# A block's edge products in one four-bank tile, with longer VectorE operations, in a graph layer with gathers

## The chip, the cores and the metric

The kernel runs on one core of a Trainium2 chip. A core has engines that run side by side, each with its own queue of instructions: TensorE (PE, matrix products; its weight loads are shown as PEld), VectorE (DVE), ScalarE (ACT), GpSimd (POOL) and SyncE (SP, which issues transfers). They wait for one another through semaphores. SBUF is the working memory; PSUM holds what PE writes, in eight banks of 512 float32 per partition. Transfers between HBM and SBUF run on 16 DMA engines. The metric is device time in microseconds (us), lower is better.

## The reference

All is float32. There are 8192 nodes of 256 features, 131072 edges with 64 attributes each, sorted by their target node, and groups of 32 nodes for attention (4 heads of 64).

```python
ea  = edge_attr @ w_e + b_e                       # 131072 x 256
msg = relu(x[src] + ea)
agg = segment_sum(msg, dst, num_segments=8192)
t   = x + agg
h_local = bn1(relu(t @ w1 + b1) @ w2 + b2 + x)
q, k, v = split(x.reshape(256, 32, 256) @ in_w.T + in_b)
attn    = softmax(q @ k.T / 8)                    # per group of 32 and head
h_attn  = bn2((attn @ v) @ out_w.T + out_b + x)
out = h_local + h_attn
out = bn3(out + relu(out @ m_w1 + m_b1) @ m_w2 + m_b2)
result = layernorm(x + out)
```

## The kernel before, in words

The edges are cut into 128 blocks of 1024 (`NB`, `BE`), the nodes into 16 chunks of 512 (`NCH`, `CH`). Blocks are numbered in the order of their edges, so block b mostly adds into the nodes around 64 b.

For a block, `gather` (L152 to L163) issues eight indirect transfers on POOL, each of which fetches 128 rows of x by the edges' source numbers into one of four buffers `xs`; it is called two blocks ahead. For the first 20 blocks (`NX`) the rows come from x itself, and PE adds the bias b_e by products with `sel` (L203); later they come from `xb`, a copy of x with b_e added. That copy is made on DVE by `copy_stream` (L639 to L647), one addition `xp` of 256 elements per partition at a time (L643), in the gaps that `copy_some` fills while the first 16 or so blocks run.

`edge_transpose` (L190) turns the edge attributes on DVE. `edge_products` (L195) multiplies them with w_e into PSUM tiles `pe` of two banks; a block needs two such tiles, one for each pair of 256-edge groups, and there are two buffers. `edge_messages` (L219) adds the gathered rows on DVE (L229, one operation of 1024 elements per tile) and takes the relu on ACT (L233). `edge_hot` (L236) compares node offsets with a row of numbers and so makes matrices of zeros and ones, in two operations of 128 elements (L241); `edge_sums` multiplies them with the messages (L250), ACT copies the sums (L268), and a second compare makes `oh2` (L279, one operation per block); `edge_place` multiplies again (L290) and adds the sums to the node tiles `xT` (L299).

The node work is written as generators. `attention_front` and `attention_back` make q, k, v, the scores, the softmax and the output of a chunk. The scores go into two tiles `pe` of the same two buffers (L482, L486); eight copies on ACT bring them to SBUF (L496). Softmax subtracts the maximum in four operations of 128 elements (L505) and multiplies with the reciprocal in four more (L512). `dense` makes the rest of a chunk: w1, w2 with an update of `hA` on DVE (L568), m_w1, m_w2, transposes and the layer norm.

The order on PE is written out by hand. Until block 104 (`TAIL`) a loop takes two blocks at a time: products and messages of the first, sums of the two blocks before, products and messages of the second, `edge_place`, and node work in between, handed out by `Work.run` by stated costs and by what is ready. From block 26 (`NV`) on, node work also stands between the sums and the second block's products; until then DVE and ACT follow the written order too, and later the scheduler orders them. From block 104 on a small planner (L803 to L855) goes block by block with an assumed time `came` at which a block's rows arrive, and picks what comes next. Its last block is taken in pieces: `first_sums` sums three of its four groups early, the last addition is cut in two, and the last `ws` copy in two halves on two engines.

At the end a check of `width` decides whether a slow general path runs; with these inputs it doesn't.

Of the kernel before, what the change touches and what calls it, by code (L numbers as in the profile page):

```python
# [24 lines left out]
NH = 4  # L25
# [47 lines left out]
def gnn_kernel(ctx: ExitStack, tc: tile.TileContext, x, src, dst, edge_attr, w, out):  # L73
# [72 lines left out]
    def bank2():  # L146
        return pps.tile([P, 2, CH], FP, name="pe", tag="pe", bufs=2)
# [47 lines left out]
    def edge_products(b):  # L195

        eaT = eaT_of.pop(b).rearrange("p (h m) r -> p h (m r)", h=NH)
        for h in range(0, NH, 2):
            pe = bank2().rearrange("p i (u c) -> p i u c", u=2)
            half = [slice(i * ED, (i + 1) * ED) for i in range(2)]  # L200
            if b < NX:
                for i, rows in enumerate(half):
                    nc.tensor.matmul(  # L203
                        pe[:, i], sel[rows, :], be[rows, None, :].to_broadcast([ED, 2, C]), start=True, stop=False, skip_group_check=True
                    )
            for u in range(2):
                for i, rows in enumerate(half):
                    nc.tensor.matmul(  # L208
                        pe[:, i, u, :], eaT[rows, h + u], we[rows, :], start=(b >= NX), stop=True, skip_group_check=True
                    )  # L210
            pe_of[b, h] = pe
# [7 lines left out]
    def edge_messages(b):  # L219

        xs = xs_of.pop(b)
        msg = msg_of[b] = epool.tile([P, NH, TJ, C], FP, name="msg", tag="msg", bufs=3)
        n = 2 if b < NB - 1 else 1
        for h in range(0, NH, 2):
            pe = pe_of.pop((b, h))
            for u in range(0, 2, n):
                hs = slice(h + u, h + u + n)
                for js in [slice(0, TJ)] if n == 2 or h + u < NH - 1 else [slice(j, j + 1) for j in range(TJ)]:
                    nc.vector.tensor_add(  # L229
                        msg[:, hs, js].rearrange("p u i c -> p i u c"), pe[:, js, u : u + n, :],  # L230
                        xs[:, hs, js].rearrange("p u i c -> p i u c"),
                    )
                    nc.scalar.activation(msg[:, hs, js], msg[:, hs, js], AF.Relu)  # L233
        between()

    def edge_hot(b):  # L236

        oh = oh_of[b] = epool.tile([P, TB, WN], FP, name="oh", tag="oh", bufs=2)
        for t0 in range(0, TB, TB // 2):
            ts = slice(t0, t0 + TB // 2)  # L240
            nc.vector.tensor_tensor(  # L241
                oh[:, ts],
                iota_n[:, None, :WN].to_broadcast([P, TB // 2, WN]),
                rel[:, b, ts, None].to_broadcast([P, TB // 2, WN]),
                ALU.is_equal,
            )
# [8 lines left out]
    def first_sums(b):  # L255
        pw = pps.tile([P, 2, C], FP, name="pw", tag="pw", bufs=1)
        group_sums(pw, 0, b, [(h, j) for h in range(NH - 1) for j in range(TJ)])
        return pw

    def edge_sums(blocks, pw=None):  # L260

        n, ws = len(blocks), []
        if pw is None:
            pw = pps.tile([P, 2, C], FP, name="pw", tag="pw", bufs=1)
            for i, b in enumerate(blocks):
                group_sums(pw, i, b, [(h, j) for j in range(TJ) for h in range(NH)])
            ws = epool.tile([P, 2, C], FP, name="ws", tag="ws", bufs=2)
            newest["ws"] = nc.scalar.copy(ws[:, :n], pw[:, :n]).ins  # L268
            ws = [ws[:, :, k * P : (k + 1) * P] for k in range(KC)]
        else:  # L270
            group_sums(pw, 0, blocks[0], [(NH - 1, j) for j in range(TJ)])
            for k, copy in enumerate((nc.vector.tensor_copy, nc.scalar.copy)):
                half = epool.tile([P, 2, C], FP, name="ws", tag="ws", bufs=2)
                copy(half[:, 0, :P], pw[:, 0, k * P : (k + 1) * P])
                ws.append(half[:, :, :P])
        oh2 = epool.tile([P, 2, WB], FP, name="oh2", tag="oh2")
        for i, b in enumerate(blocks):
            wn = window(b)
            nc.vector.tensor_scalar(oh2[:, i, :wn], iota_n[:, :wn], wrow[:, b : b + 1], None, ALU.is_equal)  # L279
        return blocks, ws, oh2  # L280

    def edge_place(blocks, ws, oh2):
# [4 lines left out]
        for i, b in enumerate(blocks):  # L287
            at, wn = first_node(b) - n, window(b)
            for k in range(KC):
                nc.tensor.matmul(  # L290
                    l2[:, k, at : at + wn], ws[k][:, i, :], oh2[:, i, :wn],
                    start=(i == 0 and k == 0), stop=(i == last), skip_group_check=True,
                )
# [168 lines left out]
    def attention_back(st, pool, bank, bank2):  # L462
# [40 lines left out]
        parts = [slice(a, a + H) for a in range(0, TN * H, H)]  # L503
        for q in parts:
            nc.vector.tensor_sub(pr3[:, q], pr3[:, q], mx[:, q, None].to_broadcast([P, H, NPG]))  # L505
# [5 lines left out]
        for q in parts:  # L511
            nc.vector.tensor_mul(pr3[:, q], pr3[:, q], sm[:, q, None].to_broadcast([P, H, NPG]))  # L512
# [126 lines left out]
    def copy_stream(i):  # L639
        for _, c, n in steps[i] if 0 <= i < len(steps) else []:  # L640
            xp = xp_of[c]
            for r in range(n * TN):
                nc.vector.tensor_add(xp[:, r, :], xp[:, r, :], be)  # L643
# [78 lines left out]
    with tc.manual_schedule(engines={PE}):  # L722
# [9 lines left out]
        for c in range(NCH):  # L732
# [10 lines left out]
            work.add(BACK, lambda s=st: s.get("front"), attention_back(st, npool, bank, bank2))  # L743
# [62 lines left out]
        summed_at, bank_free, first = {}, t, None  # L806
        work.at = [t] * len(work.streams)
        while l < NB:
# [51 lines left out]
    with tc.If(wide > 0):  # L860
# [67 lines left out]
        with tc.tile_pool(name="gfin", bufs=1) as pool, tc.tile_pool(name="gfin_ps", bufs=1, space=PSUM) as ps_pool:  # L928
# [4 lines left out]
            def gbank2():  # L933
                return ps_pool.tile([P, 2, CH], FP, name="gat2", tag="gat2", bufs=2)

            with tc.For_i(0, N, CH) as n0:
# [3 lines left out]
                for _ in attention_back(st, pool, gbank, gbank2):  # L940
# [39 lines left out]
```

## Time and profile before

| | us |
|---|---|
| median of 3 runs (1315.16 to 1317.74) | 1316.08 |
| the profiled execution | 1315.55 |
| its span, first to last instruction | 1313.8 |
| busy: PE / DVE / ACT / POOL | 1195.3 / 803.0 / 592.0 / 975.1 |

The profile is one execution. A row of the timeline gives the start and the length of an instruction (or of several equal ones, x4), its engine and line, what it writes and reads, and in square brackets the idle time of its engine before it and what ended that. A row of a group gives the count, the busy time, the mean length of one in ns, and the idle time before them. "Issue" is time in which an engine waited for nothing that the profile shows. Lengths of matmuls are modelled and overlap.

### The profile page before, as it was taken

Reading aid. Unit: us, or ns where it says so; the run is one execution under the profiler, and the core shown is the slowest. Engines: PE = TensorE matmul, PEld = TensorE weight load, DVE = VectorE, ACT = ScalarE, POOL = GpSimd, SP = SyncE. Lnnn points to the kernel's source line nnn. Section 1 sums busy time; section 2 is a strip of 40 time slices with the busy share of each in tenths; the row PEclk is TensorE's granted clock in tenths of the full one; section 3 lists DMA queues with packets and bytes.
Section 4 is the critical chain, followed back from the end, with each engine's and each line's share of the span. In section 5 each row is a group of like instructions: output and inputs, shape, how many; then the busy total and the mean of one; then the engine's idle time right before and its main releaser. Section 6 shows DMA issues by size and latency. Waiting matters only on the chain.

```text
span 1313.8 us, 21074 instructions
## 1 busy us (share of the span) xinstructions
PE 1195.3 (91%) x7683; PEld 720.5 (55%) x7683; DVE 803.0 (61%) x1635; ACT 592.0 (45%) x850; POOL 975.1 (74%) x1032
## 2 busy tenths in 40 slices
PE   5987989999999979998997998889898999989986
PEld 3544645556565545555554554545555555545664
DVE  5567665757566565755646574555647558475663
ACT  2524444454545264444544444353454445453443
POOL 6777777777777777777777777777777777777772
PEclk8988999999999999898999999989899999999999
DMA  9999985667666666756766666666667567666741
GB/s 234 287 315 281 274 219 167 178 182 194 172 176 167 170 177 161 190 160 155 195 161 184 164 177 169 157 181 171 170 169 191 147 170 196 160 167 155 193 134 50
DMA packets 148922, 240.35 MB, mean 183 GB/s; under 512 B 27950, under 2 KB 112204, under 8 KB 148044
## 3 DMA queue, kind: packets, MB, share of 16 engines
q0 software_dynamic: 49152, 134.28, 38.5%
q1 hardware_dynamic: 98572, 104.65, 29.4%
q8 instruction: 62, 1.02, 0.3%
q14 instruction: 48, 0.39, 0.1%
q10 hardware_dynamic: 1088, 0.00, 0.0%
HBM read 222.06 MB, written 16.78 MB: 182 GB/s over the span
## 4 chain that ended last, share of the span: by engine, by line
POOL 38%; PE 26%; issue 17%; DMA 9%; DVE 7%; ACT 2%; SPq 0%; DVEq 0%; POOLq 0%; ACTq 0%
POOL xs L157 38%; PE at L558 8%; DMA xs<-xb,srci 6%; PE pe L208 5%; PE pw L250 3%; PE at L455 2%; DVE msg L229 2%; PE pe L203 2%; PE l L290 2%; DMA xs<-in_x_dram,srci 2%; PE at L536 1%; DVE bd L516 1%; PE at L524 1%; PE at L469 1%; DVE y L601 1%
## 5 line engine op out<-in xcount | busy, mean ns | idle before, releaser
L157 POOL DMA_INDIRECT xs<-xb,srci x864 | 820.1, 949 | 263.2 <-issue 250.1
L233 ACT ACTIVATE msg<-msg 128x1024 f32<-128x1024 f32 (+1 forms) x259 | 269.9, 1046 | 399.2 <-DVE msg L229 395.2
L229 DVE TENSOR_TENSOR msg<-pe,xs 128x1024 f32<-128x1024 f32 (+1 forms) x259 | 306.5, 1205 | 198.0 <-PE pe L208 87.8
L208 PE MATMUL pe<-we,eaT 64*128 64x256 f32 x2048 | 266.1, 396 | 14.3 <-ACT pr L496 10.6
L208 PEld LDWEIGHTS pe<-we,eaT 64*128 64x128 f32 x2048 | 192.8, 191 | 117.6 <-issue 61.7
L157 POOL DMA_INDIRECT xs<-in_x_dram,srci x144 | 138.1, 959 | 43.9 <-issue 40.5
L250 PE MATMUL pw<-msg,oh 128*32 128x256 f32 x2048 | 130.9, 383 | 1.8 <-ACT msg L233 1.3
L558 PE MATMUL at<-hA,mw 128*128 128x512 f32 (+2 forms) x320 | 125.3, 520 | 4.8 <-DVE hA L568 4.8
L455 PE MATMUL at<-xT,inT 128*128 128x512 f32 x256 | 121.1, 599 | 3.2 <-ACT xT L445 3.2
L558 PE MATMUL at<-m,mw 128*128 128x512 f32 (+2 forms) x320 | 119.4, 517 | 0.0
L190 DVE STREAM_TRANSPOSE eaT<-ea 128x512 f32<-128x512 f32 x128 | 89.9, 702 | 22.7 <-PE pe L208 18.7
L250 PEld LDWEIGHTS pw<-msg,oh 128*32 128x32 f32 x2048 | 60.4, 109 | 64.9 <-issue 22.2
L290 PEld LDWEIGHTS l<-oh,ws 128*128 128x128 f32 x512 | 73.2, 194 | 27.4 <-issue 20.8
L290 PE MATMUL l<-oh,ws 128*128 128x160 f32 (+4 forms) x512 | 85.3, 306 | 2.4 <-ACT ws L268 1.6
L558 PEld LDWEIGHTS at<-hA,mw 128*128 128x128 f32 x320 | 55.0, 192 | 53.2 <-issue 41.2
L558 PEld LDWEIGHTS at<-m,mw 128*128 128x128 f32 x320 | 55.7, 193 | 48.0 <-issue 45.0
L455 PEld LDWEIGHTS at<-xT,inT 128*128 128x128 f32 x256 | 46.7, 190 | 57.3 <-issue 46.6
L458 ACT ACTIVATE qk<-at,vec 128x512 f32<-128x512 f32 x64 | 43.8, 685 | 73.3 <-PE at L455 73.2
L574 ACT ACTIVATE m<-at,vec 128x512 f32<-128x512 f32 (+2 forms) x80 | 47.9, 599 | 58.6 <-PE at L558 58.2
L558 PE MATMUL at<-xT,w 128*128 128x512 f32 (+2 forms) x160 | 66.0, 548 | 8.8 <-DVE xT L299 8.8
L558 PE MATMUL at<-h,w 128*128 128x512 f32 (+2 forms) x160 | 66.8, 542 | 7.6 <-ACT oT L531 5.5
L241 DVE TENSOR_TENSOR oh<-iota_n,rel 128x128 f32<-128x128 f32 x256 | 57.7, 278 | 17.7 <-PE pw L250 17.6
(113 smaller groups left out, 1199.7 us busy)
## 6 DMA issues: line engine op xcount, KB each, us to landing
ea<-in_edge_attr_dram SPq DMA_DIRECT2D x512, 128.0 KB
xs<-xb,srci POOLq DMA_INDIRECT x864
xn<-in_x_dram SPq DMA_DIRECT2D x16, 512.0 KB
out_dram<-y SPq DMA_DIRECT2D x14, 512.0 KB
xp<-in_x_dram SPq DMA_DIRECT2D x10, 512.0 KB
xb<-xp SPq DMA_DIRECT2D x10, 512.0 KB
xp<-in_x_dram SPq DMA_DIRECT2D x3, 1024.0 KB
xb<-xp SPq DMA_DIRECT2D x3, 1024.0 KB
```

What stands on the lines that cost most here:

```text
L157: nc.gpsimd.indirect_dma_start(out=xs[:, h, j, :], out_offset=None, in_=x if b < NX else xb[:, :], in_offset=bass.IndirectOffsetOnAxis(ap= ...
L190: nc.vector.transpose(eaT, ea[:, QR:].rearrange("p (g d) -> p g d", d=ED)[:, :, :QR])
L208: nc.tensor.matmul(pe[:, i, u, :], eaT[rows, h + u], we[rows, :], start=(b >= NX), stop=True, skip_group_check=True)
L229: nc.vector.tensor_add(msg[:, hs, js].rearrange("p u i c -> p i u c"), pe[:, js, u : u + n, :], xs[:, hs, js].rearrange("p u i c -> p i u c"),
L233: nc.scalar.activation(msg[:, hs, js], msg[:, hs, js], AF.Relu)
L241: nc.vector.tensor_tensor(oh[:, ts], iota_n[:, None, :WN].to_broadcast([P, TB // 2, WN]), rel[:, b, ts, None].to_broadcast([P, TB // 2, WN ...
L250: nc.tensor.matmul(pw[h * WN : (h + 1) * WN, i, :], oh_of[b][:, h * TJ + j, :], msg_of[b][:, h, j, :], start=(j == 0), stop=(j == TJ - 1), ...
L290: nc.tensor.matmul(l2[:, k, at : at + wn], ws[k][:, i, :], oh2[:, i, :wn], start=(i == 0 and k == 0), stop=(i == last), skip_group_check=True,
L455: nc.tensor.matmul(ps, inT[:, k, o * P : (o + 1) * P], xT[:, k, :], start=(k == 0), stop=(k == KC - 1))
L458: nc.scalar.activation(qk[:, o, :], ps, AF.Identity, bias=v_("in_b", o))
L558: nc.tensor.matmul(ps, wt[:, k, o * P : (o + 1) * P], act[:, k, :], start=(k == 0), stop=(k == nk - 1))
L574: nc.scalar.activation(m1[:, o, :], layer(mw1, KC, o, hA), AF.Relu, bias=v_("m_b1", o))
```

## The change

- `bank2`, a tile of two banks in two buffers, becomes `bank4`, a tile of four banks in one buffer. A block's products fill it whole; the scores of a chunk use the same tile.
- `edge_messages` adds and takes the relu of a block in one operation each of 2048 elements (the last block still by groups).
- `edge_hot` makes its compare in one operation of 256 elements. The compare for `oh2` covers both blocks of a pair in one operation with two inputs from SBUF, a `tensor_tensor`, where a `tensor_scalar` per block stood.
- Softmax's subtraction and multiplication are one operation of 512 elements each.
- The copy to `xb` adds the bias to 1024 elements at a time. `copy_some` and `between` still take one step at a call.
- In the tail `first_sums` is gone: the last block's products are issued in two halves, one before and one after the placing of the block ahead of it; its sums are issued together, its `ws` is copied at once, and its times in the planner are others.

Since readiness and stated costs decide what node work comes next, some of that work changes place on PE as well.

```diff
-    def bank2():
-        return pps.tile([P, 2, CH], FP, name="pe", tag="pe", bufs=2)
+    def bank4():
+        return pps.tile([P, 4, CH], FP, name="pe", tag="pe", bufs=1)
...
-    def edge_products(b):
-        eaT = eaT_of.pop(b).rearrange("p (h m) r -> p h (m r)", h=NH)
-        for h in range(0, NH, 2):
-            pe = bank2().rearrange("p i (u c) -> p i u c", u=2)
+    def edge_products(b, pairs=range(0, NH, 2)):
+        eaT = eaT_of[b].rearrange("p (h m) r -> p h (m r)", h=NH)
+        if b not in pe_of:
+            pe_of[b] = bank4().rearrange("p (i k) (u c) -> p i (k u) c", i=2, u=2)
+        pe = pe_of[b]
+        for h in pairs:
...
-        n = 2 if b < NB - 1 else 1
-        for h in range(0, NH, 2):
-            pe = pe_of.pop((b, h))
-            for u in range(0, 2, n):
-                hs = slice(h + u, h + u + n)
+        pe = pe_of.pop(b)
+        for hs in [slice(0, NH)] if b < NB - 1 else [slice(h, h + 1) for h in range(NH)]:
...
-        for t0 in range(0, TB, TB // 2):
-            ts = slice(t0, t0 + TB // 2)
-            nc.vector.tensor_tensor(
-                oh[:, ts],
-                iota_n[:, None, :WN].to_broadcast([P, TB // 2, WN]),
-                rel[:, b, ts, None].to_broadcast([P, TB // 2, WN]),
-                ALU.is_equal,
-            )
+        nc.vector.tensor_tensor(
+            oh,
+            iota_n[:, None, :WN].to_broadcast([P, TB, WN]),
+            rel[:, b, :, None].to_broadcast([P, TB, WN]),
+            ALU.is_equal,
+        )
...
-        for i, b in enumerate(blocks):
-            wn = window(b)
-            nc.vector.tensor_scalar(oh2[:, i, :wn], iota_n[:, :wn], wrow[:, b : b + 1], None, ALU.is_equal)
+        b, wn = blocks[0], max(window(b) for b in blocks)
+        nc.vector.tensor_tensor(
+            oh2[:, :n, :wn],
+            iota_n[:, None, :wn].to_broadcast([P, n, wn]),
+            wrow[:, b : b + n, None].to_broadcast([P, n, wn]),
+            ALU.is_equal,
+        )
...
+        four = bank4()
         for hh in range(H // 2):
-            two = bank2()
+            two = four[:, 2 * hh : 2 * hh + 2]
...
-        parts = [slice(a, a + H) for a in range(0, TN * H, H)]
-        for q in parts:
-            nc.vector.tensor_sub(pr3[:, q], pr3[:, q], mx[:, q, None].to_broadcast([P, H, NPG]))
+        nc.vector.tensor_sub(pr3, pr3, mx[:, :, None].to_broadcast([P, TN * H, NPG]))
...
-        for q in parts:
-            nc.vector.tensor_mul(pr3[:, q], pr3[:, q], sm[:, q, None].to_broadcast([P, H, NPG]))
+        nc.vector.tensor_mul(pr3, pr3, sm[:, :, None].to_broadcast([P, TN * H, NPG]))
...
-            for r in range(n * TN):
-                nc.vector.tensor_add(xp[:, r, :], xp[:, r, :], be)
-                if r == n * TN - 1:
+            for r in range(n):
+                xr = xp[:, r * TN : (r + 1) * TN, :]
+                nc.vector.tensor_add(xr, xr, be[:, None, :].to_broadcast([P, TN, C]))
+                if r == n - 1:
...
-                    times[1] = max(came[s] - 0.4, bank_free) if first is None else came[s] + 1.2
-            if p < NB and m == p:
+                    times[1] = max(came[s] + 2.2, bank_free)
+            if p < NB - 1 and m == p:
...
-                times[3] = came[m] - (2.4 if m == NB - 1 else 0.0)
+                times[3] = came[m]
...
-            elif t >= times[1] and s == NB - 1 and first is None:
-                first = first_sums(s)
-                t += 0.8
+                if l == NB - 1:
+                    edge_products(l, [2])
+                    edge_hot(l)
+                    t += 1.0
+                    p += 1
             elif t >= times[1]:
-                sums = edge_sums([s], first)
-                t += 1.2 if first is None else 0.3
+                sums = edge_sums([s])
+                t += 1.2
                 summed_at[s] = t
                 s += 1
+                if s == NB - 1:
+                    edge_products(s, [0])
+                    t += 1.0
```

More of the change, by code (lines that the diff above doesn't have):

```diff
@@ L193, in gnn_kernel @@
     pe_of, msg_of, oh_of, newest = {}, {}, {}, {}
-    def edge_products(b):
-        eaT = eaT_of.pop(b).rearrange("p (h m) r -> p h (m r)", h=NH)
-        for h in range(0, NH, 2):
-            pe = bank2().rearrange("p i (u c) -> p i u c", u=2)
-            half = [slice(i * ED, (i + 1) * ED) for i in range(2)]
+    def edge_products(b, pairs=range(0, NH, 2)):
[3 more added lines that the diff above has]
+        pe = pe_of[b]
+        half = [slice(i * ED, (i + 1) * ED) for i in range(2)]
+        for h in pairs:
             if b < NX:
@@ L253, in group_sums, with edge_sums @@
             )
-    def first_sums(b):
+    def edge_sums(blocks):
+        n = len(blocks)
         pw = pps.tile([P, 2, C], FP, name="pw", tag="pw", bufs=1)
[L257 to L264, printed above, removed]
-            for i, b in enumerate(blocks):
[L266 to L275, printed above, removed]
-        oh2 = epool.tile([P, 2, WB], FP, name="oh2", tag="oh2")
-        for i, b in enumerate(blocks):
-            wn = window(b)
-            nc.vector.tensor_scalar(oh2[:, i, :wn], iota_n[:, :wn], wrow[:, b : b + 1], None, ALU.is_equal)
+        for i, b in enumerate(blocks):
+            turns = [(h, j) for j in range(TJ) for h in range(NH)]
+            group_sums(pw, i, b, sorted(turns) if b == NB - 1 else turns)
+        ws = epool.tile([P, 2, C], FP, name="ws", tag="ws", bufs=2)
+        newest["ws"] = nc.scalar.copy(ws[:, :n], pw[:, :n]).ins
+        oh2 = epool.tile([P, 2, WB], FP, name="oh2", tag="oh2")
+        b, wn = blocks[0], max(window(b) for b in blocks)
[4 more added lines that the diff above has]
+            ALU.is_equal,
+        )
         return blocks, ws, oh2
```

32 lines of the change are left out of this document (15 added, 17 removed).

## The prediction

> **What bounds the kernel now.** I read the page first (busy shares, the 40 slices, the costliest groups), then POOL's own instructions in the timeline, then who POOL waits for, and only then the stretches around the edited lines.
>
> ```profile
> PE 1195.3 (91%) x7683; PEld 720.5 (55%) x7683; DVE 803.0 (61%) x1635; ACT 592.0 (45%) x850; POOL 975.1 (74%) x1032
> ...
> POOL 6777777777777777777777777777777777777772
> ...
> L157 POOL DMA_INDIRECT xs<-xb,srci x864 | 820.1, 949 | 263.2 <-issue 250.1
> ```
>
> PE shows the largest share, but POOL is the engine whose slices never change: seven tenths in every slice from the second to the last but one. Its 1024 gathers are one row of work, and what lies between them is "issue", not a wait. The first and the last gather in the timeline, and POOL's waits:
>
> ```profile
> 4.39 1.10 POOL L157 DMA_INDIRECT xs<-in_x_dram,srcd  x1 [2.80 <-issue]
> ...
> 1289.18 0.94 POOL L157 DMA_INDIRECT xs<-xb,srci  x1 [0.30 <-issue]
> ```
> ```profile
> POOL xs L157 <- issue: 297.7, 969, 2.8
> ...
> POOL xs L157 <- DVE msg L229: 2.1, 7, 0.3
> ```
>
> From 4.39 to 1289.18 are 1284.8 us for 1023 steps. An undisturbed step is 0.95 us of work and 0.30 us of issue, 1.25 us; 1023 of them make 1278.8. So the span of 1313.8 is 4.4 us of start, 1278.8 us of gathers at full rate, 6.0 us by which single gathers ran long, and 24.6 us from the last gather's start to the end. The longest wait of POOL for a message buffer is 0.3 us, which is the issue gap itself: no buffer ever held it up. Work taken off DVE, ACT or PE in the body is therefore worth nothing by itself; the time moves only through (a) gathers that run long, (b) a buffer that comes free too late, (c) the tail.
>
> **(a) Which gathers run long.** Rows of the timeline, DVE and POOL, in pairs:
>
> ```profile
> 54.94 0.42 DVE L643 TENSOR_TENSOR xp<-xp,be 128x256 f32<-128x256 f32 x1
> 55.15 1.03 POOL L157 DMA_INDIRECT xs<-in_x_dram,srci  x1 [0.30 <-DVE msg L229]
> ...
> 82.17 0.42 DVE L643 TENSOR_TENSOR xp<-xp,be 128x256 f32<-128x256 f32 x1
> 82.28 1.14 POOL L157 DMA_INDIRECT xs<-in_x_dram,srci  x1 [0.30 <-issue]
> ...
> 185.52 0.42 DVE L643 TENSOR_TENSOR xp<-xp,be 128x256 f32<-128x256 f32 x1
> 185.74 1.02 POOL L157 DMA_INDIRECT xs<-in_x_dram,srci  x1 [0.30 <-issue]
> ...
> 858.20 0.90 DVE L505 TENSOR_TENSOR pr<-pr,mx 128x128 f32<-128x128 f32 x4
> 858.70 1.01 POOL L157 DMA_INDIRECT xs<-xb,srci  x1 [0.30 <-issue]
> ...
> 1262.07 1.23 DVE L229 TENSOR_TENSOR msg<-pe,xs 128x1024 f32<-128x1024 f32 x1 [0.47 <-DMA xs<-xb,srci]
> 1262.95 0.94 POOL L157 DMA_INDIRECT xs<-xb,srci  x1 [0.30 <-issue]
> ```
>
> And the DVE groups by shape:
>
> ```profile
> L229 DVE TENSOR_TENSOR msg<-pe,xs 128x1024 f32<-128x1024 f32 x254 | 303.6, 1218 | 196.9 <-PE pe L208 87.8 <-DMA xs<-xb,srci 60.4 <-ACT m L574 15.6
> L241 DVE TENSOR_TENSOR oh<-iota_n,rel 128x128 f32<-128x128 f32 x256 | 57.7, 278 | 17.7 <-PE pw L250 17.6
> L643 DVE TENSOR_TENSOR xp<-xp,be 128x256 f32<-128x256 f32 x64 | 24.6, 417 | 0.0
> L279 DVE TENSOR_SCALAR oh<-iota_n,wrow 128x160 f32<-128x160 f32 x80 | 21.8, 310 | 0.0
> L505 DVE TENSOR_TENSOR pr<-pr,mx 128x128 f32<-128x128 f32 x64 | 14.6, 283 | 0.3
> L512 DVE TENSOR_TENSOR pr<-pr,sm 128x128 f32<-128x128 f32 x64 | 14.6, 287 | 0.4
> L229 DVE TENSOR_TENSOR msg<-pe,xs 128x512 f32<-128x512 f32 x3 | 2.0, 683 | 0.1
> ```
>
> From 512 to 1024 elements L229 grows by 0.535 us, 1.045 ns an element; 256 elements stream for 0.27 us. The L643 of 82.17 is done streaming at about 82.47 (0.27 and some 0.03 of start). The gather that starts inside it, at 82.28, is 0.19 us longer than 0.95: it waits until just then. The same sum gives 0.09 and 0.08 for the pairs at 55.15 and 185.74, and 0.08 and 0.07 were seen. Over the trace, 15 gathers start inside an L643 (first and last above), 14 of them over 0.03 us late, 0.12 us on average; the four pieces of L505 at 858.20 do it too. The L229 at 1262.07 has one input in PSUM, and the gather inside it takes 0.94: none of the 222 that start inside an L229 is late. So a gather that begins while DVE streams an operation with both inputs in SBUF waits for that operation's end. An operation that streams for L catches a start with chance L/1.25 and then costs L/2 on average: L²/2.5. For L643 that is 64 x 0.27²/2.5 = 1.9 us, against 15 x 0.12 = 1.8 seen.
>
> [...]
>
> **The change, part by part.** Cost goes with L², so k operations merged into one cost k times as much:
> - The copy to xb: 64 of 256 become 16 of 1024 elements, L 1.07: 16 x 1.07²/2.5 = 7.3, in place of 1.9: +5.5 us, all by block 16.
> - Softmax's subtraction and multiplication: 128 of 128 become 32 of 512, L 0.535: 3.7 in place of 0.9: +2.7.
> - The compare for oh: 256 of 128 become 128 of 256: 3.7 in place of 1.8: +1.9.
> - The compare for oh2: a tensor_scalar per block becomes a tensor_tensor with two SBUF inputs, for 51 pairs of about 300 elements (L 0.31) and 26 single blocks of about 110: 2.1, in place of about 0.4 seen at L279: +1.7.
>
> Sum +11.8. No two-SBUF operation of 512 or 1024 elements is in this trace. Below: a hit costs what it costs now whatever L is; the copy's 14 hits (16 x 1.07/1.25) then cost 0.12 each, softmax's 14, oh's 27 and oh2's 14 about 0.08 each, 6.1 in all where 5.0 stand now: +1. Above: every start inside waits out the full L, twice the mean: 33.6 in place of 5.0, +29. The rows lie on the line of "until the end" to 0.02 us, so I take +11.8; where the hits fall is chance, some 2 us either way.
> - The message addition and relu: one of 2048 in place of two of 1024, 2.29 and about 1.9 us. One input is in PSUM, so no gather pays. DVE saves 0.15 us a block, hidden.
>
> **(b) Buffers.** One tile of four banks means that the next block's products wait for the whole addition. Rows of PE, DVE, ACT and POOL in the stretch where PE is the late engine:
>
> ```profile
> 82.19 3.68 PE L524 MATMUL at<-bd,vn 128*64 128x128 f32 x32 [6.34 <-DVE bd L516]
> ...
> 95.93 1.23 DVE L229 TENSOR_TENSOR msg<-pe,xs 128x1024 f32<-128x1024 f32 x1 [0.50 <-DMA xs<-in_x_dram,srci]
> ...
> 97.68 1.13 PE L203 MATMUL pe<-be,sel 64*128 64x512 f32 x4
> ...
> 153.87 2.06 PE L486 MATMUL pe<-qk 64*128 64x128 f32 x32
> ...
> 155.08 3.00 ACT L496 COPY pr<-pe 32x256 f32<-32x256 f32 x8 [5.04 <-PE pe L486]
> ...
> 156.62 1.13 PE L203 MATMUL pe<-be,sel 64*128 64x512 f32 x4 [0.69 <-ACT pr L496]
> ...
> 184.38 1.23 DVE L229 TENSOR_TENSOR msg<-pe,xs 128x1024 f32<-128x1024 f32 x1 [0.50 <-PE pe L208]
> ...
> 187.06 0.95 POOL L157 DMA_INDIRECT xs<-in_x_dram,srci  x1 [0.30 <-DVE oh L279]
> ...
> 201.49 1.22 DVE L229 TENSOR_TENSOR msg<-pe,xs 128x1024 f32<-128x1024 f32 x1 [0.44 <-PE pe L208]
> ...
> 207.13 0.95 POOL L157 DMA_INDIRECT xs<-xb,srci  x1 [0.30 <-issue]
> ```
>
> A gather needs the buffer of four blocks before. Block 14's last addition ends at 185.61 and the gather of block 18 starts at 187.06: 1.45 us to spare, the least of all blocks; block 16 has 4.4 (202.71 to 207.13). What is added until block 14: in each of five pairs the second block's products start when the addition ends, 95.93 + 2.29 = 98.2 in place of 97.68, 0.6 us, together 3; at scores all eight copies must be done (158.08) where products started at 156.62, 1.5 us each, twice in full; the addition itself ends 1.1 us later; minus about 1.5 where PE waited for softmax anyway (6.34 us before 82.19) and softmax is shorter. Sum 5.6, so 4.2 past the spare (bounds 0 and 9); block 16 comes to some 8, 3.6 past. But POOL is itself later by then: the copy's +5.5 and some 0.5 of the other parts. The larger covers the smaller: I count 0.4 for the cases in which it doesn't. If (a) were nothing, (b) would cost its 4.2. From block 26 on other work is planned between the two products of a pair, which covers the addition: nothing.
>
> **(c) Tail.**
>
> ```profile
> 1291.92 0.42 DVE L229 TENSOR_TENSOR msg<-pe,xs 128x256 f32<-128x256 f32 x1 [0.76 <-DMA xs<-xb,srci]
> ...
> 1295.60 0.33 DVE L299 TENSOR_TENSOR xT<-l,xT 128x160 f32<-128x160 f32 x1 [1.07 <-PE l L290]
> ...
> 1299.58 2.10 PE L558 MATMUL at<-hA,mw 128*128 128x128 f32 x16
> ...
> 1309.02 0.41 DVE L613 TENSOR_SCALAR y<-y,mv,rstd 128x256 f32<-128x256 f32 x1
> ```
>
> In the new order DVE does one hA update of the third quarter ahead of the last two additions, and PE does the second half of block 127's products, w1, w2 and one group of mw1 ahead of all the block's sums. I put the last addition's end at about 1293.9 (now 1292.34) and the last xT addition at 1297.1 (now 1295.60): +1.5. Behind it stand 42 products where 46 stood, two passes of 0.13 us each: -0.9. One ws copy for two saves 0.2, counted already. Net +0.6, bounds -1 and +2.5.
>
> **Sum.** 1315.55 + 11.8 + 0.4 + 0.6 = 1328.4 for the profiled execution, which is 0.5 under the median of the runs shown; against the median 1328.9. I forecast 1329 (+1.0%). No change means within 0.2%, 2.6 us.
>
> **Rivals.**
> - A: a hit costs no more than now (+1, above), and (b) decides: 1316.1 + 1 + 4.2 + 0.6 = 1322. For it: no long two-SBUF operation was seen. Against: lateness follows the end of the operation to 0.02 us. Chance 0.14.
> - B: (b) is larger than I make it, POOL stalls by 12 or more before block 20, and 5.8 of the later port costs and 0.6 of tail come on top: 1335. It decides only past the 6 us by which POOL is late itself. Nothing in the spare times forbids it; PE's order is close to the old one, which speaks against. Chance 0.06.
> - C, the other side: late gathers go by the number of operations and not by their length. the 448 of them, with the oh2 compares some 580, become 253, the lateness of 5 us falls to 2, and with block 14 still in its spare the time is 1316.1 - 3 + 0.6 = 1313.7. It decides if a long operation lets a gather in after a fixed time. Against: the latenesses beside L643 reach 0.23 us and those beside L505 0.12, as their lengths do. Chance 0.04.
> - D: all of it hidden, the floor of 1278.8 plus 6.0 stays and the tail gives 0.6: 1316.7. It needs both (a) and (b) wrong. Chance 0.04.
>
> **How the numbers follow.** My forecast has 0.72, its own range 1325 to 1333. The range 1321 to 1335 reaches over A's time to B's and leaves out 0.18: C, D and the outer parts of the other three. Slower: the forecast, A and B, 0.92; no change D, 0.04; faster C, 0.04.
>
> **What would show it.** Right: mean gathers of well over 0.949 us, with single ones near 2 us beside the 1024-element copies, and none beside the message addition; POOL's last start near 1301. Wrong: gathers as short as now (A, D), or rows in which POOL waits several us for msg before 210 us (B). For (c): the last xT addition 8 us behind the last gather's start, now 6.4.

## The result, and the profile after

The changed kernel takes 1350.28 us in the median of 4 runs (1348.89 to 1351.72), the kernel before 1315.72 in the same session: a ratio of 1.0257, 95% interval 1.0244 to 1.0269. The forecast was 1329 with a range to 1335. The direction was right, the size was not: 34.6 us lost where 13 were forecast.

The profiled span is 1349.9 us, 36.1 more than before. The page after, its busy shares, POOL's slices, the head of the chain and POOL's two groups of gathers:

```profile
PE 1207.9 (89%) x7683; PEld 732.7 (54%) x7683; DVE 770.4 (57%) x1184; ACT 568.0 (42%) x723; POOL 984.2 (73%) x1032
...
POOL 7777567767777777777777777777777777777770
...
PE 49%; POOL 16%; DVE 11%; issue 9%; DMA 9%; ACT 5%; SPq 0%; DVEq 0%; POOLq 0%; ACTq 0%
...
L157 POOL DMA_INDIRECT xs<-xb,srci x864 | 823.8, 953 | 270.0 <-issue 247.7
L157 POOL DMA_INDIRECT xs<-in_x_dram,srci x144 | 142.9, 993 | 57.9 <-issue 39.0
```

POOL's row of slices now has a dent (a 5) in the fifth slice, and the chain that ended last runs through PE for 49% of the span and through POOL's gathers for 16%. The group of the first blocks (from `in_x_dram`) is where it went: gathers of 993 ns in the mean, and 57.9 us idle before them, of which issue explains only 39.0. Who ended POOL's idle time, and its first and last gather:

```profile
POOL xs L157 <- issue: 293.6, 956, 2.6
POOL xs L157 <- DVE msg L227: 24.5, 12, 9.0
```
```profile
4.22 1.10 POOL L157 DMA_INDIRECT xs<-in_x_dram,srcd  x1 [2.62 <-issue]
...
158.05 1.68 POOL L157 DMA_INDIRECT xs<-in_x_dram,srci  x1 [9.04 <-DVE msg L227]
...
1318.95 0.95 POOL L157 DMA_INDIRECT xs<-xb,srci  x1 [0.30 <-issue]
```

L227 is the addition that was L229. The longest wait for a message buffer was 0.3 us; it is 9.0 now, at the gather of 158.05. POOL's 1024 gathers and the pauses between them split the whole difference. "Late" is the sum of what each gather took over 0.947 us, "gaps" the sum of what each pause took over 0.302, "tail" the time from the last gather's start to the end of the span; all kernels of this study stand in one table:

| kernel | ratio to before (95%) | late | gaps | tail |
|---|---|---|---|---|
| before | 1 | 6.0 | 1.1 | 24.6 |
| after | 1.0257 (1.0244 to 1.0269) | 15.4 | 21.7 | 31.0 |
| e1: after, scores' products first | 1.0133 (1.0113 to 1.0152) | 18.7 | 5.5 | 26.6 |
| e2: after, old short operations | 1.0289 (1.0271 to 1.0306) | 6.2 | 25.0 | 39.1 |
| e3: both of these | 1.0122 (1.0105 to 1.0138) | 5.7 | 21.3 | 25.3 |
| e4: before, only the long operations | 1.0093 (1.0076 to 1.0110) | 18.9 | 3.1 | 23.3 |
| f5: e3, addition and relu in halves | 1.0129 (1.0113 to 1.0146) | 8.0 | 18.6 | 26.6 |
| f6: before, only the new tail | 0.9993 (0.9984 to 1.0003) | 6.1 | 1.1 | 23.5 |
| f7: before, only the one relu | 1.0029 (1.0017 to 1.0041) | 6.2 | 2.6 | 29.1 |
| f8: before, only the copy to xb in 1024 | 1.0032 (1.0019 to 1.0045) | 13.2 | 0.9 | 24.8 |

The sums are taken from rows as the timeline prints them, to 0.01 us. In the profiled executions of e1, e3 and e4 an undisturbed gather took 949 ns in the median, in the others 946; both print as 0.95, so in these three some 2 us of the gaps column are no waits. POOL's pauses over 0.35 us, less the issue, come to 20.8 us after, 2.4 in e1, 24.1 in e2, 18.1 in e3, 17.9 in f5, 1.4 in f7, and to nothing in before, e4, f6 and f8.

After less before: 9.4 late, 20.6 in gaps, 6.4 in the tail, and 0.2 less at the start, together 36.2 of the 36.1. Step (a) had forecast 11.8, step (b) 0.4, step (c) 0.6.

Where TensorE loses its time shows in the timeline of the first chunk's scores, PE and ACT, after (L475 are the score products, L485 the copies of scores, L231 the relu, L443 products of the next chunk):

```profile
58.37 1.91 ACT L231 ACTIVATE msg<-msg 128x2048 f32<-128x2048 f32 x1 [3.78 <-DVE msg L227]
58.39 1.16 PE L475 MATMUL pe<-qk 64*128 64x128 f32 x16 [0.53 <-DVE msg L227]
60.19 1.47 ACT L485 COPY pr<-pe 32x256 f32<-32x256 f32 x4
61.71 1.16 PE L475 MATMUL pe<-qk 64*128 64x128 f32 x16 [2.16 <-ACT pr L485]
62.92 1.49 ACT L485 COPY pr<-pe 32x256 f32<-32x256 f32 x4 [1.26 <-PE pe L475]
64.14 6.66 PE L443 MATMUL at<-xT,inT 128*128 128x512 f32 x12
```
```profile
PE pe L475 <- ACT pr L485: 31.9, 16, 2.7
PE pe L475 <- DVE msg L227: 15.1, 11, 3.9
```

The second half of a chunk's scores goes into banks 2 and 3 of the tile. Its 16 products end at 62.87 and could have started at 59.5. They started at 61.71, when ACT had copied the first half out of banks 0 and 1, and those copies had stood behind the relu of 1.91 us. Before, all 32 products ran in one go (2.06 us at 153.87), since each half had a tile of its own. This wait comes once in each of the 16 chunks, 31.9 us in all. Nothing in the prediction speaks of it. A stretch of the trace from 64 to 66 us also shows a granted clock of 0.50, in which the first of the twelve products of L443 run; they take 6.66 us, and in e1 below, without the pause, 5.34.

### The profile page after: what moved, and what is told of

Read it like the earlier page. It is cut to its first block, busy times and chain, and to the rows that moved or that the text cites. A ratio compares the mean times of both kernels' runs of the same rounds, so it can differ in the third digit from the quotient of the medians.

```text
span 1349.9 us, 20465 instructions
## 1 busy us (share of the span) xinstructions
PE 1207.9 (89%) x7683; PEld 732.7 (54%) x7683; DVE 770.4 (57%) x1184; ACT 568.0 (42%) x723; POOL 984.2 (73%) x1032
## 4 chain that ended last, share of the span: by engine, by line
PE 49%; POOL 16%; DVE 11%; issue 9%; DMA 9%; ACT 5%; SPq 0%; DVEq 0%; POOLq 0%; ACTq 0%
POOL xs L157 16%; PE at L544 14%; PE pe L210 10%; PE at L443 6%; DVE msg L227 5%; PE pw L246 4%; DMA xs<-xb,srci 4%; PE l L278 3%; PE at L522 3%; ACT msg L231 2%; PE at L457 2%; PE pe L475 2%; ACT pr L485 2%; PE at L510 1%; PE pe L205 1%
## 5 line engine op out<-in xcount | busy, mean ns | idle before, releaser
L227 DVE TENSOR_TENSOR msg<-pe,xs 128x2048 f32<-128x2048 f32 (+1 forms) x132 | 293.4, 2225 | 223.1 <-PE pe L210 112.2
L231 ACT ACTIVATE msg<-msg 128x2048 f32<-128x2048 f32 (+1 forms) x132 | 245.2, 1859 | 270.1 <-DVE msg L227 270.1
L210 PE MATMUL pe<-we,eaT 64*128 64x256 f32 x2048 | 266.5, 398 | 15.6 <-DVE msg L227 10.8
L157 POOL DMA_INDIRECT xs<-in_x_dram,srci x144 | 142.9, 993 | 57.9 <-issue 39.0
L246 PE MATMUL pw<-msg,oh 128*32 128x256 f32 x2048 | 126.8, 383 | 5.6 <-ACT msg L231 4.9
L443 PE MATMUL at<-xT,inT 128*128 128x512 f32 x256 | 124.1, 612 | 4.4 <-ACT xT L433 4.4
L259 ACT COPY ws<-pw 128x512 f32<-128x512 f32 (+1 forms) x77 | 39.4, 511 | 186.6 <-PE pw L246 186.5
L190 DVE STREAM_TRANSPOSE eaT<-ea 128x512 f32<-128x512 f32 x128 | 89.9, 703 | 22.7 <-PE pe L210 18.9
L278 PEld LDWEIGHTS l<-oh,ws 128*128 128x128 f32 x512 | 76.0, 200 | 27.2 <-issue 21.2
L475 PE MATMUL pe<-qk 64*128 64x128 f32 x512 | 46.4, 332 | 47.1 <-ACT pr L485 31.9
L443 PEld LDWEIGHTS at<-xT,inT 128*128 128x128 f32 x256 | 47.7, 194 | 60.2 <-issue 50.7
L287 DVE TENSOR_TENSOR xT<-l,xT 128x352 f32<-128x352 f32 (+14 forms) x107 | 43.0, 423 | 52.6 <-PE l L278 50.3
```

The lines of the kernel that those rows point to most:

```text
L157: nc.gpsimd.indirect_dma_start(out=xs[:, h, j, :], out_offset=None, in_=x if b < NX else xb[:, :], in_offset=bass.IndirectOffsetOnAxis(ap= ...
L190: nc.vector.transpose(eaT, ea[:, QR:].rearrange("p (g d) -> p g d", d=ED)[:, :, :QR])
L210: nc.tensor.matmul(pe[:, i, u, :], eaT[rows, u], we[rows, :], start=(b >= NX), stop=True, skip_group_check=True)
L227: nc.vector.tensor_add(msg[:, hs, js].rearrange("p u i c -> p i u c"), pe[:, js, hs, :], xs[:, hs, js].rearrange("p u i c -> p i u c"),)
L246: nc.tensor.matmul(pw[h * WN : (h + 1) * WN, i, :], oh_of[b][:, h * TJ + j, :], msg_of[b][:, h, j, :], start=(j == 0), stop=(j == TJ - 1), ...
L278: nc.tensor.matmul(l2[:, k, at : at + wn], ws[:, i, k * P : (k + 1) * P], oh2[:, i, :wn], start=(i == 0 and k == 0), stop=(i == last), ski ...
```

## Experiments

Two theories. T1: TensorE, held up by that wait and by the one tile, became the late engine, and POOL waits for buffers. T2: only the longer VectorE operations cost, by late gathers.

### e1: all score products of a chunk before the first copy

```diff
                         start=True,
                         stop=True,
                     )
+        for hh in range(H // 2):
+            two = four[:, 2 * hh : 2 * hh + 2]
             two4 = two.rearrange("p s (t k) -> p s t k", t=TN)
```

> The changed kernel with one edit: all 32 score products of a chunk are issued before the first copy of scores, so that the second half of the products no longer waits for ScalarE's copies of the first half in the shared tile. T1 (TensorE, held up by that wait, became the late engine and POOL waits for its buffers): the rows that end TensorE's idle time at the scores with ScalarE's copies (31.9 us in 16 waits) go, the lag of the additions behind their gathers shrinks again after block 20, most of the 20.8 us of POOL's gaps over the issue go and the tail returns towards 24.6; late gathers stay near 15.4. Time 1325 to 1335. T2 (only the longer VectorE operations cost, by late gathers; the rest of the wait is moved elsewhere, to the whole-tile addition and relu): 1345 to 1351.

It took 1335.1 us against 1318.31 for the kernel before, timed beside it, so of the 2.6% lost the order of 16 products gives half back. TensorE's rows of the same place, and POOL's waits:

```profile
56.97 2.06 PE L475 MATMUL pe<-qk 64*128 64x128 f32 x32 [0.53 <-DVE msg L227]
58.95 1.13 PE L278 MATMUL l<-oh,ws 128*128 128x96 f32 x8
59.92 5.34 PE L443 MATMUL at<-xT,inT 128*128 128x512 f32 x12
```
```profile
POOL xs L157 <- DVE msg L227: 4.6, 7, 1.8
```

The 32 products are one row again, and POOL's waits for a message buffer fall from 24.5 to 4.6 us. The twelve products of L443 take 5.34 us where they took 6.66 behind the wait: more on that below. The time is at the upper edge of T1's range (1325 to 1335) and far from T2's. Late gathers did not stay near 15.4, against what T1 said; they rose to 18.7, which fits a POOL that runs at its own pace again while the long operations go on.

### e2 and e3: the old lengths, without and with that order

```diff
-            for r in range(n):
-                xr = xp[:, r * TN : (r + 1) * TN, :]
-                nc.vector.tensor_add(xr, xr, be[:, None, :].to_broadcast([P, TN, C]))
+            for r in range(n * TN):
+                nc.vector.tensor_add(xp[:, r, :], xp[:, r, :], be)
...
-        nc.vector.tensor_sub(pr3, pr3, mx[:, :, None].to_broadcast([P, TN * H, NPG]))
+        for q in parts:
+            nc.vector.tensor_sub(pr3[:, q], pr3[:, q], mx[:, q, None].to_broadcast([P, H, NPG]))
```

(and the same for softmax's multiplication and the compares for oh and oh2.)

> The changed kernel with only its longer two-SBUF-input VectorE operations put back to the old lengths (copy to xb 256, softmax 128, oh 128, oh2 by block as tensor_scalar); the four-bank tile, its one addition and relu and the new tail stay. T1: late gathers fall from 15.4 to about 6 us, but POOL waits for buffers by as much more, since TensorE sets the pace: the time gains 0 to 4 us, 1346 to 1351. T2: the 9.4 us of lateness are gained in full, 1340 to 1342.

> Both edits of the two kernels before. T1: without the scores' wait POOL is the bound again, so the short operations now gain what they did not gain alone: late gathers 6 us, gaps 0 to 4 us, tail 25 to 27, time 1316 to 1323. T2: 1340 to 1342, as with short operations alone.

e2 took 1356.38 us: late gathers fell to 6.2 as both theories said, and nothing was gained; by the ratio it lost a little (1.0289 against 1.0257, 1.0271 to 1.0306 against 1.0244 to 1.0269), which neither theory had: T1 said a gain of 0 to 4 us. The gaps rose to 25.0 and the tail to 39.1. VectorE's copy to xb takes 24.6 us in place of 19.5 there, and softmax's two lines 29.2 in place of 22.1; that TensorE's waits are longer for it, as the additions stand behind these operations in VectorE's queue, is argued and not shown alone. T2 is out.

e3 took 1334.97, and here T1 was wrong too: it said 1316 to 1323. With the scores' wait gone and the short operations back, POOL still waits 20.0 us for message buffers:

```profile
POOL xs L157 <- DVE msg L227: 20.0, 7, 8.1
```

e1 and e3 take the same time with opposite make-up, 18.7 late and 5.5 of gaps against 5.7 and 21.3. Two things can let TensorE catch up in e1, and no run parts them: POOL loses time to late gathers, and VectorE's long operations are shorter in sum. The scores' wait was half the loss; the change holds something else that makes TensorE late by as much again.

### e4 and f8: the long operations alone

e4 is the kernel before with the reverse of the diff above; f8 has only its first part, the copy to xb.

> The kernel before with only the longer VectorE operations (copy to xb 1024, softmax 512, oh 256, one oh2 compare for both blocks); tiles of two banks, two additions and two relus a block and the old tail stay. By the length-squared rule of the prediction, and by the 9.4 us that were seen in the changed kernel: 1325 to 1328, in single late gathers of up to 0.7 us, with no gap at a buffer over 1 us. If lateness does not go with length: 1315 to 1318. If the longer operations themselves hold up the products or the softmax (so that part of the gaps is theirs): 1330 to 1340.

> The kernel before with only the copy to xb in 16 operations of 1024 elements in place of 64 of 256, once more at the higher clock (at 0.826, with TensorE the bound, it gained 1.6%: the additions for xb are shorter on VectorE and late gathers cost nothing there). The length-squared law: +5.5 us, 1.004, late gathers 11.5 us in sum with single ones up to 1.07 us late. With the extra VectorE time saved on TensorE's chain nothing changes, as POOL is the bound. If a hit costs what it cost at 256 elements: 1.000 to 1.001.

e4 took 1330.62 against 1318.31, +12.3; late gathers rose by 12.9, and the tail fell by 1.3; the 2.0 more in the gaps column are no waits (no pause of POOL there is over 0.32 us). In us that is in the third of the expected ranges (1330 to 1340: the long operations hold up products or softmax), but the kernel before, timed beside it, was itself 2.6 us slower than beside the changed kernel; with no wait of POOL, nothing is left of that third case. Single gathers were up to 1.04 us late, more than the 0.7 expected. It is step (a)'s +11.8, alone and in its size. f8 gave 1.0032 of 1316.13, +4.2, and 7.2 more of lateness in its profiled run, for the 5.5 of the copy's term. (What its expectation says of a clock of 0.826 is taken up at the end of this section.) A pair of rows of f8, VectorE's addition of 1024 elements and the gather that starts inside it:

```profile
47.95 1.22 DVE L644 TENSOR_TENSOR xp<-xp,be 128x1024 f32<-128x1024 f32 x1
48.13 1.86 POOL L157 DMA_INDIRECT xs<-in_x_dram,srci  x1 [0.30 <-issue]
```

At the 1.045 ns an element that the prediction read from L229, 1024 elements stream for 1.07 us; with 0.03 of start the operation is done streaming at 49.05 by this estimate, and the gather is 0.91 late: 48.13 and 0.92 is 49.05. The same sum for the 15 gathers that start inside one gives 8.8 us, and 8.55 were seen. So a late gather waits until the operation is done streaming at four times the length too.

### f5, f6 and f7: one tile, one relu, or the tail

Theory S: the one tile itself, whose last read the next products wait for. Theory R: the length of the one relu, behind which ACT's copies queue. f5 is e3 with

```diff
-        for hs in [slice(0, NH)] if b < NB - 1 else [slice(h, h + 1) for h in range(NH)]:
+        for hs in [slice(0, 2), slice(2, NH)] if b < NB - 1 else [slice(h, h + 1) for h in range(NH)]:
```

f6 is f5 with two tiles of two banks again for products and scores, which leaves the kernel before with the new tail. f7 is the kernel before with one relu behind both additions:

```diff
-                    nc.scalar.activation(msg[:, hs, js], msg[:, hs, js], AF.Relu)
+                    if n == 1:
+                        nc.scalar.activation(msg[:, hs, js], msg[:, hs, js], AF.Relu)
+        if n == 2:
+            nc.scalar.activation(msg, msg, AF.Relu)
```

> The kernel with scores first and short operations (1.0122 of the kernel before), and in it the addition and the relu of a block again in two halves of 1024, still in one tile of four banks; once more, since in the first run TensorE's clock was 0.826 and TensorE the bound in every kernel. Theory R, the length of the one relu on ScalarE: POOL's gaps over the issue fall from 21.3 to under 8 us, 1.001 to 1.006 of the kernel before. Theory S, the one tile, whose last read the next block's products wait for: gaps 15 us or more, 1.009 to 1.014.

> The kernel before with nothing but the new tail, once more at the higher clock. Both theories: gaps under 1.5 us, late gathers 6 us, the last addition to xT 8 us behind the last gather's start; 0.9995 to 1.002 of the kernel before (step (c): +0.6 us, bounds -1 and +2.5).

> The kernel before with one relu of 2048 elements behind both additions in place of two of 1024, once more at the higher clock. Theory R: block 14 overruns its spare, POOL waits 5 us or more in all, 1.004 to 1.008 of the kernel before. Theory S: 1.000 to 1.002.

f5 stays at 1.0129 with 18.6 us of gaps (17.9 of waits, where e3 had 18.1), f6 is at 0.9993 with 1.1. Between the two stands nothing but the tile (with two of them the order of a chunk's scores matters no more, as it has nothing to wait for): one of four banks costs 1.4%, 18 us, with short operations, short relus and scores in the better order. POOL's waits in f5, and the row in f7 that says what the relu alone does there:

```profile
POOL xs L157 <- DVE msg L227: 20.3, 9, 7.1
```
```profile
188.25 0.94 POOL L157 DMA_INDIRECT xs<-in_x_dram,srci  x1 [1.70 <-DVE msg L229]
```

f7 lies between the theories. The gather that needs block 14's buffer waits 1.70 (1.40 over the issue), as its spare of 1.45 us is used up. The larger part of what its profiled run lost is 4.5 us in the tail; there the granted clock was 0.66 from 1295 to 1300 us, where it was 1.00 before (twelve matmuls of the last sums took 3.21 us at 1295.52, and 2.35 before), and how much of the tail is the clock and how much the long relu stays open. f6 misses its expectation in one point: its last addition to xT came 6.57 us behind the last gather's start, not 8. S is the main cause, R a small one.

Why the one tile costs 18 us where step (b) summed up 5.6 shows in TensorE's windows from 10 us to the end of block 14's addition (the columns: the stretch, its length, busy time of PE, PEld, DVE, ACT and POOL with counts, granted clock, DMA share, GB/s); before, after, e1 and e3:

```profile
10.00:185.60 175.60, 150.71 (x1008) 92.65 (x1010) 114.46 (x254) 70.92 (x107) 133.38 (x139) 0.94 0.98 279
```
```profile
10.00:205.40 195.40, 159.68 (x1013) 97.71 (x1012) 106.04 (x155) 67.39 (x93) 138.98 (x140) 0.90 0.88 252
```
```profile
10.00:193.60 183.60, 153.03 (x1012) 93.10 (x1011) 105.24 (x153) 67.53 (x93) 140.10 (x141) 0.93 0.94 268
```
```profile
10.00:203.30 193.30, 157.34 (x1013) 95.84 (x1012) 112.74 (x239) 67.16 (x93) 134.89 (x140) 0.91 0.87 255
```

About a thousand matmuls (1008 to 1013 records) take 6.6 us longer in e3 than before, 9.0 longer after and 2.3 longer in e1. In short stretches of the traces before and after, the granted clock reads 1.00 or 0.50 (after: 1.00 from 60 to 63 us, 0.50 from 64 to 66), and its mean in the window gives an estimate of what it cost: at 0.942 of 175.6 us TensorE lost 10.2 us of full speed before, after 18.8 (0.904 of 195.4), in e3 17.1 and in e1 11.9. That is 8.5, 6.8 and 1.7 us more than before, near the 9.0, 6.6 and 2.3 by which the matmuls are longer. The idle time beside them is 24.9 us before (175.60 less 150.71), 30.6 in e1, 36.0 in e3, 35.7 after. So block 14 was late by 8.0 to 19.8 us where the pauses were 5.7 to 11.1 us longer: a pause counted 1.4 to 1.8 times here, itself and what the matmuls were longer by. Who ended the pauses, before and in e3, from 10 us to the same point:

```profile
PE pe L203 <- DVE msg L229: 5.4, 1, 5.4
...
PE at L455 <- ACT xT L445: 3.2, 4, 1.9
...
PE pe L203 <- ACT pr L496: 0.7, 1, 0.7
```
```profile
PE at L441 <- ACT xT L431: 6.6, 2, 3.8
PE pe L205 <- DVE msg L227: 6.2, 6, 3.6
PE pe L205 <- ACT pr L485: 5.1, 2, 3.1
```

After scores, the next products wait until all eight copies are done (5.1 us in place of 0.7); the next chunk's first product waits for a copy of xT that stands behind the relu (6.6 in place of 3.2; with short relus, in f5, still 5.2, so the relu's length explains the smaller part); the products wait for the whole addition (6.2 in six pauses in place of 5.4 in one). How the 18 us divide between the products' wait and the copies' wasn't separated by a kernel: the two share the tile.

### The same four kernels on a slower chip

e5 to e8 were the kernels of f5 to f8 on another chip, with a mean granted clock of 0.81 to 0.83; the kernel before took 2017.59 us there in the median.

> The kernel with scores first and short operations (1334.97 us), and in it the addition and the relu of a block again in two halves of 1024, still in one tile of four banks. What is left there is 21.3 us of POOL's gaps over the issue. Theory R, the length of the one relu: what queues behind it on ScalarE (the copy of the transposed nodes, for which TensorE waits 3.78 us where it waited 1.87) gets its place back; gaps fall under 8 us, time 1319 to 1325. Theory S, the one tile: the next block's products still wait until the last read of the tile; TensorE's wait at L205 for the addition stays, gaps 15 us or more, time 1330 to 1336.

> The same with two tiles of two banks for products and scores: the kernel before with nothing but the new tail. Both theories: gaps under 1.5 us, late gathers 6 us. For the tail, step (c) of the prediction says +0.6 (bounds -1 and +2.5), the last addition to xT 8 us behind the last gather's start: 0 to 2 us over the kernel before.

> The kernel before with one edit: one relu of 2048 elements behind both additions in place of two of 1024; two tiles, two additions, old lengths, old tail. Theory R: the copies behind the relu come 1 to 2 us late in each chunk, block 14 (1.45 us to spare) overruns and POOL waits 5 us or more in all: before + 5 to + 10. Theory S: before + 0 to + 2.

> The kernel before with one edit: the copy to xb in 16 operations of 1024 elements in place of 64 of 256. The length-squared law of step (a): +5.5 us, all before 210 us, in some 14 gathers that start inside one, none over 1.07 us late. If lateness has a cap near 0.73 us, as in the changed kernel: +4 to +5. If a hit costs what it cost at 256 elements: 0 to +1.

They gave 1.0113 (1.0001 to 1.0224), 1.0011 (0.9965 to 1.0056), 1.0025 (0.9985 to 1.0064) and 0.9839 (0.9746 to 0.9931). None of the expectations in us applies: POOL waited 632.2 us for message buffers in e6. The expectations of f5 and f8 read this as a TensorE that is the bound because its clock is low. The page of e6 says otherwise, busy shares and chain:

```profile
PE 1396.8 (70%) x7683; PEld 797.5 (40%) x7683; DVE 806.2 (40%) x1634; ACT 593.6 (30%) x850; POOL 972.7 (49%) x1032
...
PE 48%; another core or an unknown queue 23%; issue 11%; ACT 8%; DVE 8%; DMA 1%; POOL 0%; DVEq 0%; SPq 0%; ACTq 0%
```

TensorE stands idle for 30% of the span, where it was 9% in the kernel before above, and 23% of the chain is put down to another core or an unknown queue, which no page of the faster chips has. In the windows above more idle time went with a lower mean clock (24.9 us and 0.94 before, 35.7 us and 0.90 after), so the low mean here may as well follow from the idle time as cause it. What held the engines up on this chip isn't shown, and these four runs decide nothing between R and S. Nor is e8's gain explained: its verdict is unclear, and its executions had clocks of 0.830 to 0.833 where the kernel before had 0.818 to 0.832. That the merged copy pays where TensorE is the bound is a guess that no run here tests.

## Why the prediction was wrong

**What bounds the kernel** was read rightly for before: gathers at full rate, no buffer late. The sentence drawn from it, that work in the body moves the time only through (a), (b) and (c), held. What was wrong is how much (b) could take.

**(a) held.** Forecast +11.8; e4 shows +12.9 of lateness alone, the changed kernel 9.4; in e1, where POOL hardly waits, it is 12.7 again. By lines, after: 11 gathers in the copies were late by 6.2 us in all (forecast 7.3), 9 in softmax by 2.1 (3.7), 19 in oh by 2.0 (3.7), 12 in oh2 by 2.0 (2.1). None of the lower or upper bounds was near: a hit waits until the operation is done streaming. In the pair below that is 114.41 (113.31 and 1.10), and the gather is 0.73 late: 113.67 and 0.73 is 114.40.

```profile
113.31 1.22 DVE L630 TENSOR_TENSOR xp<-xp,be 128x1024 f32<-128x1024 f32 x1
113.67 1.68 POOL L157 DMA_INDIRECT xs<-in_x_dram,srci  x1 [0.30 <-issue]
```

VectorE's own time fell with the longer operations: the copy to xb took 19.5 us after, in 16 of 1024 elements, where it took 24.6 in 64 of 256.

**(b) is the step that failed**: "Sum 5.6, so 4.2 past the spare", and then 0.4 counted. Block 14's addition ended 19.8 us later (205.4 for 185.61), and the gaps came to 20.6. The prediction's own sign for B, POOL waiting several us for msg before 210 us, is what the trace shows. The sum looked at block 14, the one with the least to spare; the longest stall, the 9.04 us at 158.05, is for the buffer of block 10, which had 3.2 us to spare before and whose addition ended 14.3 us later. Who ended TensorE's pauses after, from 10 us to the end of block 14's addition:

```profile
PE at L510 <- DVE bd L502: 7.5, 2, 6.5
PE pe L205 <- DVE msg L227: 6.7, 6, 4.1
PE pe L475 <- ACT pr L485: 5.9, 3, 2.2
PE at L443 <- ACT xT L433: 4.4, 3, 3.8
...
PE pe L205 <- ACT pr L485: 1.6, 1, 1.6
```

The terms that the sum held were not too small. The products' waits for the addition grew by 2.4 us (6.7 and 1.1 at the scores, where 5.4 stood; 3 were forecast), those for all eight copies by 0.9 (3 forecast), and the wait for softmax fell by 1.0 (1.5 forecast). Three terms were missing:
- The scores' second half behind the copies of its first half, and these behind the relu: 5.9 us on TensorE by block 14, 31.9 over the run, 1.2% of the time by after against e1. The text counted only what waits behind the scores. It treated the slices of one tile as two tiles, while it counted the tile as one for the products.
- ACT's queue: the copy of xT, for which TensorE paused 4.4 us where 3.2 stood (6.6 in e3).
- The clock. Beside 11 us more of pauses about the same matmuls lasted 9 us longer, 8.5 of them by the granted clock.

"The larger covers the smaller" fits e1 and e3, but with (b) the larger. "From block 26 on ... nothing" was wrong as well. Before, the lag of a block's last addition behind its last gather falls from 27.8 us at block 14 to 2.3 at block 58; after, it is 15.2 at block 58, and at block 127 it is 10.2 where 1.8 stood before. In e1, without the scores' wait, it is 7.4 and 5.9; so that wait, which comes back in every chunk, eats much of what TensorE had to spare. (The lag is from the gather's end to the addition's start.)

**(c)** was forecast at +0.6 and came to +6.4. The order alone (f6) gives 23.5 in place of 24.6, -1.1; its last addition to xT stands 6.57 us behind the last gather's start (1289.13 to 1295.70), not 8:

```profile
1295.70 0.33 DVE L283 TENSOR_TENSOR xT<-l,xT 128x160 f32<-128x160 f32 x1 [2.86 <-PE l L274]
```

With the one tile it is 8.14 (e3), near the 8 that was forecast; the last addition itself starts 1.5 us later behind the last gather there than in f6. The tail is then 25.3, +0.7. The other 5.7 after go with the lag that (b) left at block 127, 10.2 us where e3 has 3.3. (The 4 products fewer, at two passes of 0.13 us each, make 1.0 and not the 0.9 of the sum, which changes nothing. The trace before counts 16 passes for a block's 8 sums, and 16 of L558 take 2.10 us at 1299.58.)

**Rivals.** B had the right place and the right engine, with a price too small: 12 us by block 20 and 1335. The gaps to 210 us were 14.1, a further 6.9 came before 420, and the tail's 6.4 stood in no rival. A fell with the lengths of late gathers, C with it (fewer operations, more lateness), D with both.

**No version beats the kernel before** where its time could be explained. The new tail alone is the same within what can be measured. How the cost of the one tile divides between the products' wait and the scores' copies stays open.

## What to carry to other kernels

Before a tile is merged, list every writer and reader of the merged tile, and count for each writer the last reader of any part that stands ahead of it; slices of one tile may be ordered like one, as the two halves of the scores were here (31.9 us in 16 waits). Ask of the engine that is not the bound how much it has to spare per round, not only at its worst moment: a wait of 2 us in each of 16 chunks does nothing where it stands and takes away the catching up that everything behind it needs, and more when the clock falls behind it, as it did here behind the wait at 61.71 (0.50 for 3.4 us). And a merge that saves VectorE time can still cost: the merged copy lost 0.3% here (f8), with POOL as the bound.

## What the hardware showed that wasn't expected

TensorE's pauses cost more than their length: 5.7, 11.1 and 10.8 us more of them up to block 14 went with 8.0, 17.7 and 19.8 us of delay there (e1, e3, after). Behind the pause of 2.16 us at 61.71 the twelve products of L443 took 6.66 us, without the pause (e1) 5.34; behind a pause of 3.78 for xT twelve took 7.26 in e3 where 5.88 stood before behind 1.87 (two and ten products, 126.23 to 132.11). The granted clock was lower where the pauses were longer: its mean over about the same work was 0.94 before, with 24.9 us of idle time, and 0.90 after, with 35.7, and behind the pause at 61.71 stands a stretch of 3.4 us at 0.50, from 63.4 us on. TensorE had been idle for 1.7 of the 3.4 us ahead of it. What decides when the clock falls, and for how long, isn't shown by these runs.

The law of late gathers (a gather that starts inside an operation with both inputs in SBUF waits until that is done streaming) held to within 0.03 us for the hits in the copy at 1024 elements after and in f8, four times the longest operation on which it had been read.
